# A block of the output projection in seven products of 128x128, and a new order of the instructions from the first load to the fourth block

## The chip, the core and the metric

The kernel runs on one core of one Trainium2 chip. The metric is the device time of one execution in microseconds (us). It was run three times; the median is 998.61 us (997.31 to 998.91). One execution was also taken with the profiler. All arithmetic is fp32.

## The reference

One cross-attention block. x has 16 batches of 1024 rows of 512 features, the context 16 batches of 64 rows.

```python
def _ada_ln(x, c, W_ss, b_ss):
    h = (x - mean(x)) / sqrt(var(x) + 1e-5)
    scale, bias = split(silu(c) @ W_ss + b_ss, 2)
    return (1 + scale)[:, None, :] * h + bias[:, None, :]

q      = _ada_ln(x,   cond, Wss_q,  bss_q)  @ Wq  + bq      # 16 heads of 32
k, v   = _ada_ln(ctx, cond, Wss_kv, bss_kv) @ Wkv + bkv
attn   = softmax(q @ k.T / sqrt(32))                        # per head, 64 keys
return x + ((attn @ v) @ Wp + bp)
```

## The kernel before, in words

**Blocks.** The rows of x are worked on in NB = 32 blocks of 512 rows (two per batch). The context is worked on once, in two groups of eight batches, "A" and "B", between the first blocks. Every block passes through these steps; the letters in brackets are the engines.

- `load_x` (SP issues the DMA), `q_stats` (VectorE: a batch-norm statistic and its aggregation per 128 rows, L287 and L288), `q_scale` (ScalarE and GpSimd: five and four instructions on 4 numbers a partition), `hidden` (ScalarE, L344: normalises), `turn` (VectorE, L374: 32x32 transposes), `move` (16 DMAs of 64 KB), `scale_features` (ScalarE, L459: the modulation).
- The query projection `query_product(i, 1..7)` (TensorE, L551). A 512x512x512 product would be eight products of 256x256x256. By Winograd's form of Strassen's method it is seven of them, `seven()`, with sums of weight blocks made once (`column_sums`) and sums of feature blocks made for every block (`feature_sums`, GpSimd, L510). Two of the seven, numbers 1 and 7, are cut in the same way a second time from the fifth block on, into seven products of 128x128x128: `quarter_products` in two parts of four and three (TensorE, L622), `feature_quarters` (GpSimd, L598 to L600, three sums), `quarter_copies` (ScalarE, L633) and `quarter_adds` (VectorE, L639 to L641). `query_out` (ScalarE, L662) and `query_added` (VectorE, L669) carry the results to SBUF.
- `score_products(i, 0)` and `(i, 1)` (TensorE, L755, 32x32 products into two PSUM tiles of two banks each, pool `ps_s`, which has two such tiles in all), `maximum` (VectorE, L772) and `copied` (ScalarE, L781), both reading these tiles; `maxima` (VectorE), `subtract` (GpSimd, L814: a whole 128x2048 tile), `weights` (ScalarE, the exponentials, L836), `swapped` (DMA), `again` (ScalarE, L861), `total` (GpSimd, L902), `row_total` and `inverse_rows` (VectorE, L907 and L922, then five small DMAs), `spread_rows` (VectorE, L957).
- `mix` (TensorE, L1002: weights times values), `divided` (VectorE, L981).
- The output projection `product(i, 1..7)` (TensorE, L1155): again seven products of 256x256x256, with the weight sums `WT` made once (`weight_sums`) and sums of rows for every block (`row_sum(i, 0..3)`, GpSimd, L1120 to L1127). Products 1, 6, 5, 3 add up in one PSUM bank, products 2, 4, 7 in another: `biased(i, 2)` and `biased(i, 3)` (ScalarE, L1099) set the banks to the bias, `output_seed` (ScalarE, L1108) copies the first bank into the second after product 1, and `added(i, n)` (VectorE, L1288) adds a bank to the residual rows; after products 3 and 4 the rows are stored by DMA.

A product of 256x256x256 is four fp32 matmuls of a 128x128 stationary block with 256 moving columns; the profile counts two instructions for each, eight in all. A cut product is seven fp32 matmuls of 128 moving columns, fourteen instructions.

**Order.** There is no scheduler: `tc.manual_schedule()` (L71) leaves every engine's queue in the order of the calls written out from L1297 on. Waits are put in where one instruction's bytes depend on another's, and every engine takes its own queue strictly in order. The calls are a way in (L1297 to L1757), a loop over blocks 3 to 29 (L1759), and a tail for blocks 30 and 31 (L1876 on). In the loop `i` is the block whose scores are made; `a = i - 1`, `b = i - 2`, `n = i + 1`, `f = i + 2`.

Some helpers stand in the file but are hardly used or not at all: `lowered(i, e)` (L816: half of the subtraction of the second score tile, on VectorE straight from PSUM; used for block 30 only), `subtract_half` (L822), `q_stats_two` and `q_square_mean` (L323, L336), and the family `inner_weight_sums`, `inner_biased`, `inner_quarters`, `inner_products`, `inner_copies`, `inner_adds` (L1181 to L1265).

Of the kernel before, what the change touches and what calls it, by code (L numbers as in the profile page):

```python
# [15 lines left out]
P = 128  # L16
# [4 lines left out]
def cross_attention_block(  # L21
# [18 lines left out]
    nc = tc.nc  # L40
# [5 lines left out]
    NC = H // P  # L46
# [141 lines left out]
    def load_projection(again=False):  # L188
        src = w_p.rearrange("(c p) o -> p c o", p=P)
        if again:  # L190
            nc.sync.dma_start(w_p_sb[:, : NC // 2, :], src[:, : NC // 2, :])
        else:
            nc.sync.dma_start(w_p_sb, src)
# [1104 lines left out]
    for _ in range(WARM):  # L1298
        nc.tensor.transpose(warm[:, :P], ident, ident)
    load_x('A')  # L1300
    load_scale_shift('kv', w_ss_kv, 0)
    q_stats('A', (0,))
    q_stats('A', (1,))
    q_stats('A', (2,))
    load_scale_shift('kv', w_ss_kv, 1)
    q_stats('A', (3,))
    q_scale('A')
    load_context_weights(1, 0)
    hidden('A', (0,))
    biases()  # L1310
    load_context_weights(0, 1)
    scale_shift_rows('kv', 0)
    scale_shift_taken('kv', 0)
    turned_features('A', 0)
    hidden('A', (2,))
    hidden('A', (1,))
    turned_features('A', 1)
    hidden('A', (3,))
    scale_shift('kv', 2 * NC, 0)
    turned_features('A', 2)  # L1320
    turned_features('A', 3)
    modulated('A', 0, 1, nc.vector)
    load_context_weights(0, 0)
    modulated('A', 0, 0, nc.scalar)
    scale_shift_rows('kv', 1)
    scale_shift_taken('kv', 1)
    load_x(0)
    modulated('A', 0, 0, nc.vector)
    modulated('A', 0, 1, nc.scalar)
    load_scale_shift('q', w_ss_q, 0)  # L1330
    column_sums('k', w_k_sb, w_k_sums, (0,))
    scale_shift('kv', 2 * NC, 1)
    load_scale_shift('q', w_ss_q, 1)
    column_sums('k', w_k_sb, w_k_sums, (1,))
    modulated('A', 1, 0, nc.scalar)
    column_sums('k', w_k_sb, w_k_sums, (2,))
    modulated('A', 1, 0, nc.vector)
    context_product('A', 'v', 1)
    context_product('A', 'k', 2)
    modulated('A', 1, 1, nc.vector)  # L1340
    load_x('B')
    modulated('A', 1, 1, nc.scalar)
    feature_sums('A', nc.vector, (0,))
    context_product('A', 'k', 1)
    feature_sums('A', nc.vector, (1,))
    context_out('A', 'k', 1)
    feature_sums('A', nc.vector, (2,))
    q_stats(0, (0,))
    context_out('A', 'k', 2)
    context_product('A', 'v', 2)  # L1350
    context_product('A', 'k', 6)
    q_stats(0, (1,))
    q_stats(0, (2,))
    scale_shift_rows('q', 0)
    q_stats(0, (3,))
    q_scale(0)
# [702 lines left out]
```

## Time and profile before

| | |
|---|---|
| median of the runs | 998.61 us |
| profiled execution, its own time | 996.79 us |
| its span | 994.9 us, so 1.9 us lie around the span |
| granted TensorE clock | 1.0 |
| TensorE busy | 982.9 us, 99% |
| VectorE busy | 898.5 us, 90% |
| GpSimd busy | 893.0 us, 90% |
| ScalarE busy | 780.2 us, 78% |
| DMA, written and read in all | 165.52 MB, mean 166 GB/s |
| one round of the loop (185.63 to 214.16 us and 470.85 to 499.37 us) | 28.5 us |
| loop over blocks 3 to 29 | 149.4 to 927.2 us |

The profiled execution took 1.8 us less than the median. Where an engine is nearly always busy, its idle time in a stage and what ended it are read from the waits; where it is not, busy shares say little. "PE" is TensorE, "PEld" its weight loads, "DVE" VectorE, "ACT" ScalarE, "POOL" GpSimd, "SPq" the queue of SyncE that issues DMAs. Neighbouring instructions on VectorE, ScalarE and GpSimd overlap by a little, so the spacing of their starts is often shorter than their duration.

### The profile page before, as it was taken

What the parts mean: (1) busy time and instruction counts of PE and PEld (TensorE: products, weight loads), DVE (VectorE), ACT (ScalarE), POOL (GpSimd) and SP (SyncE); (2) the same over time, 40 slices, a digit from 0 to 9 for tenths busy, and PEclk for the clock granted to TensorE, in tenths of its full rate; (3) what the DMA queues carried; (4) which work ended last, traced back from release to release, by engine and by line L of the source; (5) the groups of instructions that cost most, each with busy time, mean ns of one, the idle gap of its engine ahead of it and who ended that gap; (6) DMA issues with size and microseconds to landing.
All of it is one profiled execution on the core that took longest, in us unless ns stands there. A gap on an engine that the chain in (4) does not pass through costs nothing.

```text
span 994.9 us, 20661 instructions
## 1 busy us (share of the span) xinstructions
PE 982.9 (99%) x7501; PEld 767.7 (77%) x7501; DVE 898.5 (90%) x1326; ACT 780.2 (78%) x1169; POOL 893.0 (90%) x695
## 2 busy tenths in 40 slices
PE   8999999999999999999999999999999999999997
PEld 7888777777777777777777778777787787777776
DVE  7687899999999999999999999999999999987995
ACT  3878868888888888888888888888888888876540
POOL 2687999999999999999999999999999999999861
PEclk9999999999999999999999999999999999999999
DMA  9765755555656555556655555565555556544323
GB/s 316 257 173 148 172 161 143 156 161 171 190 181 181 164 152 164 142 180 191 184 178 159 160 154 151 182 188 181 178 152 172 149 155 182 148 135 131 116 90 108
DMA packets 114885, 165.52 MB, mean 166 GB/s; under 512 B 34872, under 2 KB 46160, under 8 KB 112864
## 3 DMA queue, kind: packets, MB, share of 16 engines
q1 hardware_dynamic: 114400, 163.67, 55.2%
q8 instruction: 60, 0.98, 0.4%
q0 software_dynamic: 384, 0.54, 0.2%
q14 instruction: 41, 0.34, 0.1%
HBM read 79.21 MB, written 34.60 MB: 114 GB/s over the span
## 4 chain that ended last, share of the span: by engine, by line
PE 94%; POOL 1%; DMA 1%; SPq 1%; DVE 1%; issue 1%; DVEq 0%; ACT 0%; POOLq 0%
PE pp L1155 37%; PE pq L551 29%; PE pq L622 10%; PE ps L755 7%; PE po L1002 6%; PE pk_A L551 1%; PE pv_B L551 1%; PE pk_B L551 1%; PE pv_A L551 1%; DMA w_k_sb<-in_L_xcond_Wkv_dram 1%; PE pp_0b L1155 1%; POOL sum L902 0%; SPq L166 0%; SPq L143 0%; DVE m L772 0%
## 5 line engine op out<-in xcount | busy, mean ns | idle before, releaser
L814 POOL TENSOR_TENSOR s<-s,mb 128x2048 f32<-128x2048 f32 x63 | 286.1, 4563 | 16.5 <-DVE mb L801 9.2
L1155 PE MATMUL pp<-w_p_sb,ot 128*128 128x256 f32 x756 | 178.9, 380 | 0.2 <-DVE ot L981 0.2
L772 DVE TRANSPOSE_TENSOR_REDUCE m<-ps 128x32 f32<-128x1024 f32 x128 | 152.3, 1226 | 10.0 <-PE ps L755 9.7
L781 ACT COPY s<-ps 128x1024 f32<-128x1024 f32 x126 | 127.4, 1013 | 41.8 <-PE ps L755 36.9
L1155 PEld LDWEIGHTS pp<-w_p_sb,ot 128*128 128x128 f32 x756 | 141.2, 190 | 21.9 <-issue 1.9
L662 ACT ACTIVATE qt<-pq,bias_t 128x256 f32<-128x256 f32 x256 | 107.5, 474 | 52.9 <-PE pq L622 27.8
L902 POOL TENSOR_TENSOR sum<-s,p 128x2048 f32<-128x2048 f32 x30 | 136.4, 4547 | 1.6 <-ACT p L836 1.6
L1288 DVE TENSOR_TENSOR r<-pp,r 128x512 f32<-128x512 f32 x188 | 123.6, 669 | 14.2 <-ACT xt L459 6.8
L551 PE MATMUL pq<-xt,w_q_sums 128*128 128x256 f32 x512 | 123.8, 385 | 0.0
L1155 PE MATMUL pp<-WT,ot 128*128 128x256 f32 x508 | 122.0, 383 | 0.0
L551 PEld LDWEIGHTS pq<-xt,w_q_sums 128*128 128x128 f32 x512 | 95.2, 190 | 34.3 <-issue 22.6
L1155 PE MATMUL pp<-WT,s 128*128 128x256 f32 x504 | 119.6, 380 | 0.7 <-DVE r L1288 0.5
L861 ACT ACTIVATE s<-s 32x2048 f32<-32x2048 f32 x60 | 114.6, 1910 | 1.5
L1155 PEld LDWEIGHTS pp<-WT,ot 128*128 128x128 f32 x508 | 94.2, 190 | 17.8 <-issue 3.0
L1155 PEld LDWEIGHTS pp<-WT,s 128*128 128x128 f32 x504 | 91.5, 191 | 11.9 <-DVE r L1288 1.4
L344 ACT ACTIVATE x<-x,rstdq 128x512 f32<-128x512 f32 x128 | 94.8, 807 | 1.0 <-POOL rstdq L305 0.9
L459 ACT ACTIVATE xt<-xt,ss_q 128x512 f32<-128x512 f32 x124 | 93.9, 807 | 0.5 <-DMA xt<-ht 0.3
L981 DVE TENSOR_TENSOR ot<-po,vb 128x1024 f32<-128x1024 f32 x64 | 75.5, 1219 | 18.8 <-PE po L1002 17.4
L287 DVE BATCH_NORM_STATS2 bs<-x 128x6 f32<-128x512 f32 x128 | 85.3, 666 | 0.0
L510 POOL TENSOR_TENSOR xt_sums<-xt 128x512 f32<-128x512 f32 x64 | 81.2, 1268 | 1.4 <-ACT xt L459 0.9
L374 DVE STREAM_TRANSPOSE ht<-x 128x512 f32<-128x512 f32 x124 | 77.7, 679 | 4.3 <-ACT x L344 2.2
L907 DVE TRANSPOSE_TENSOR_REDUCE lt<-sum 128x64 f32<-128x2048 f32 x31 | 71.6, 2310 | 6.2 <-POOL sum L902 3.9
(221 smaller groups left out, 1957.6 us busy)
## 6 DMA issues: line engine op xcount, KB each, us to landing
x<-in_x_dram SPq DMA_DIRECT2D x32, 1024.0 KB, 5.4
r<-in_x_dram SPq DMA_DIRECT2D x32, 1024.0 KB, 5.7
out_dram<-r SPq DMA_DIRECT2D x62, 512.0 KB, 5.0
xt<-ht SPq DMA_DIRECT2D x488, 64.0 KB, 2.0
p<-s SPq DMA_DIRECT2D x60, 256.0 KB, 3.8
wss_kv<-in_L_xcond_Wss_kv_dram SPq DMA_DIRECT2D x4, 512.0 KB, 7.2
wss_q<-in_L_xcond_Wss_q_dram SPq DMA_DIRECT2D x4, 512.0 KB, 10.5
vr<-ltd SPq DMA_DIRECT2D x128, 8.0 KB, 1.8
```

The source lines that it names most:

```text
L344: nc.scalar.activation(dst, src, AF.Identity, bias=rstd[:, 1, j : j + 1], scale=rstd[:, 0, j : j + 1])
L459: nc.scalar.activation(xt[:, :, c, :], xt[:, :, c, :], AF.Identity, scale=ss["q"][:, c, b : b + 1], bias=ss["q"][:, NC + c, b : b + 1],)
L551: nc.tensor.matmul(out_, lhsT=lhsT, rhs=rhs, start=new and m == 0 and c == 0, stop=c == HC - 1, skip_group_check=True,)
L622: nc.tensor.matmul(qa["q", k][:, q * P : (q + 1) * P], lhsT=lhsT, rhs=rhs, start=first and q == 0, stop=True, skip_group_check=True,)
L662: nc.scalar.activation(dst, src, AF.Identity, bias=bq_t[:, o : o + 1])
L772: nc.vector.tensor_reduce(m_tiles[i][:, z, 2 * e : 2 * e + 2, :], s_banks[i, z][e].rearrange("p r (j a) -> p r j a", a=32), AX.X, ALU.max, ...
L781: nc.scalar.copy(s_tiles[i, z][:, 2 * e : 2 * e + 2, :], s_banks[i, z][e])
L814: eng.tensor_tensor(s_tiles[i, z], s_tiles[i, z], mb_tiles[i], ALU.subtract)
L861: nc.scalar.activation(s_tiles[i, 0][at + 32 : at + 64], raw_tiles[i][at : at + 32], AF.Exp, scale=SCALE)
L902: nc.gpsimd.tensor_tensor(t, s_tiles[i, 0], s_tiles[i, 1], ALU.add)
L1155: nc.tensor.matmul(to, lhsT=rows[:, c, t * P : (t + 1) * P], rhs=cols[:, c, :], start=n == 2 and (i, 2) not in seeded and t == 0 and c == ...
L1288: nc.vector.tensor_add(r, a, r)
```

## The change

1. **Projection's product 1 is cut.** For blocks 2 to 28 (27 of the 32) `product(i, 1)` with `biased(i, 2)` gives way to `inner_biased`, `inner_quarters`, `inner_products` (two parts), `inner_copies` and `inner_adds`: seven products of 128x128x128. The sums of weight blocks are made once by `inner_weight_sums(1)` in the way in. One of them is written over a 128x128 block of the weights in place, so for blocks 29 to 31, which keep the whole product, `load_projection(again=True)` fetches that block (64 KB) once more in the tail.
2. **Work is moved between engines in every block from 3 on (statistics: from block 7 on).** Half of the subtraction of the second score tile goes from GpSimd to VectorE (`lowered(a, 0)`), which also saves one of the four `copied` on ScalarE; GpSimd keeps the other half (`subtract_half(a, 1, 1)`). The row statistics of two of the four row tiles go from VectorE to ScalarE (`q_stats_two`, two activations each whose elements are also summed up) with a small multiplication on GpSimd (`q_square_mean`).
3. **The order is another one throughout.** The way in is rewritten: the two halves of the keys' weights are loaded ahead of the first half of the values' weights, the first product of the context is the keys' product 1 in place of the values' product 1, and the order of blocks 0 to 4 is new. The loop now runs over blocks 5 to 27 and begins in the middle of a block's work; `load_x(i + 4)` and the statistics of block `i + 3` stand where those of `i + 5` and `i + 4` stood. The last four blocks are written out in the tail.

The functions of point 1, which were in the file already:

```python
def inner_weight_sums(v):              # POOL, once; s(2) is the weight block (1, 0) itself
    tt(s(0), w(1, 0), w(1, 1), ALU.add)
    tt(s(1), s(0), w(0, 0), ALU.subtract)
    tt(s(2), w(0, 0), w(1, 0), ALU.subtract)
    tt(s(3), w(0, 1), s(1), ALU.subtract)
    if v == 1:
        b = const.tile([P, HO], F32, tag="first", name="first_bias")
        nc.gpsimd.tensor_copy(b[:, :P], b_first[:, :P])
        tt(b[:, P:], b_first[:, P:], b_first[:, :P], ALU.subtract)
def inner_biased(i, v):                # ACT, two copies of 128x256
    nc.scalar.copy(acc[k][:, :HO], inner_bias[v])
    nc.scalar.copy(acc[k][:, HO:], zero.to_broadcast([P, HO]))
def inner_quarters(i, v, eng=nc.gpsimd):   # POOL; t shares its buffer with s2 of row_sum(i, 2)
    tt(t[:, 0:2], x[:, 1, 0:2, :], x[:, 0:2, 0, :], ALU.subtract)
    tt(t[:, 2], x[:, 1, 1, :], t[:, 0], ALU.subtract)
    tt(t[:, 3], x[:, 0, 1, :], t[:, 2], ALU.subtract)
def inner_products(i, v, first):       # PE
    todo = ((0, w(0, 0), x[:, 0, 0, :]), (2, s(0), t[:, 0]), (1, s(2), t[:, 1]), (3, s(1), t[:, 2])
            ) if first else ((0, w(0, 1), x[:, 0, 1, :]), (2, s(3), x[:, 1, 1, :]), (1, w(1, 1), t[:, 3]))
def inner_copies(i, v):                # ACT, 128x256
    nc.scalar.copy(inner_tiles[i, v][:, 0:2], a[:, :, 0, :])
def inner_adds(i, v):                  # DVE
    tt(t[:, 2], a[:, 3 * P :], t[:, 0], ALU.add)
    tt(both_, both_, t[:, 2:3].to_broadcast([P, 2, P]), ALU.add)
    tt(a[:, 3 * P :], a[:, P : 2 * P], t[:, 1], ALU.add)
def q_stats_two(i, ts):                # ACT, two per row tile
    nc.scalar.activation(junk, x, AF.Identity, scale=1.0 / H, accum_out=mv[:, t, 0:1])
    nc.scalar.activation(junk, x, AF.Square, scale=-1.0, bias=mv[:, t, 0:1], accum_out=mv[:, t, 1:2])
```

The core of the diff:

```diff
     def load_projection(again=False):
         if again:
-            nc.sync.dma_start(w_p_sb[:, : NC // 2, :], src[:, : NC // 2, :])
+            nc.sync.dma_start(w_p_sb[:, 0, P : 2 * P], src[:, 0, P : 2 * P])
...
-    load_context_weights(1, 0)
     hidden('A', (0,))
-    biases()
-    load_context_weights(0, 1)
+    hidden('A', (2,))
     scale_shift_rows('kv', 0)
     scale_shift_taken('kv', 0)
+    load_context_weights(0, 0)
     turned_features('A', 0)
...
+    scale_shift_rows('kv', 1)
+    load_context_weights(0, 1)
+    biases()
     hidden('A', (1,))
+    scale_shift('kv', 2 * NC, 0)
+    scale_shift_taken('kv', 1)
...
+    load_context_weights(1, 0)
+    scale_shift('kv', 2 * NC, 1)
+    modulated('A', 0, 0, nc.vector)
+    modulated('A', 1, 0, nc.vector)
...
-    context_product('A', 'v', 1)
-    context_product('A', 'k', 2)
...
     context_product('A', 'k', 1)
...
+    context_product('A', 'v', 2)
...
+    context_product('A', 'k', 2)
...
+    weight_quarter_sums(7)
+    inner_weight_sums(1)
...
-    for i in range(3, NB - 2):
+    for i in range(5, NB - 4):
         a, b, n, f = (i - 1, i - 2, i + 1, i + 2)
```

The loop after the change in full, its conditions (which hold in every round that they matter in) left out; several calls to a line:

```python
quarter_products(i, 7, True); lowered(a, 0); product(i-3, 3); product(i-3, 4); subtract(a, zs=(0,))
scale_features(n, (0,)); spread_rows(b); added(i-3, 3); scale_features(n, (1,)); mix(b)
quarter_copies(i, 7); quarter_adds(i, 7); added(i-3, 4); query_out(i, 6); hidden(f, (2,))
inner_biased(b, 1); weights(a, 0); quarter_products(i, 7, False); subtract_half(a, 1, 1); turn(f, (0,))
load_residual(a); feature_quarters(n, 1); weights(a, 1); query_product(i, 5); divided(b, (0,)); divided(b, (1,))
turn(f, (1,)); inner_quarters(b, 1); query_out(i, 7); total(a); turn(f, (2,)); q_stats_two(i+3, (0,))
inner_products(b, 1, True); inner_copies(b, 1); query_added(i, 5); turn(f, (3,)); load_x(i+4); inner_adds(b, 1)
query_product(i, 4); query_product(i, 3); query_added(i, 4); move(f, ks=(0,)); q_stats_two(i+3, (1,))
row_sum(b, 0); inner_products(b, 1, False); query_out(i, 3); scale_features(n, (2,)); output_seed(b)
q_stats(i+3, (2,)); swapped(a); scale_features(n, (3,)); score_products(i, 0); quarter_products(n, 1, True)
copied(i, 0, 1); q_stats(i+3, (3,)); q_square_mean(i+3, range(2)); row_total(a); quarter_copies(n, 1)
move(f, ks=(1,)); maximum(i, 0, 0); row_sum(b, 2); move(f, ks=(2,)); product(b, 2); quarter_adds(n, 1)
feature_sums(n, (0,)); move(f, ks=(3,)); product(b, 6); q_scale(i+3); copied(i, 0, 0); maximum(i, 0, 1)
hidden(i+3, (3,)); feature_sums(n, (1,)); feature_sums(n, (2,)); inverse_rows(a); quarter_products(n, 1, False)
added(b, 2); query_seed(n); score_products(i, 1); query_product(n, 2); added(b, 6); maximum(i, 1, 1)
maximum(i, 1, 0); biased(b, 3); row_sum(b, 3); maxima(i); again(a, 0); hidden(i+3, (0,)); row_sum(b, 1)
query_out(n, 2); product(b, 5); product(b, 7); added(b, 7); feature_quarters(n, 7); again(a, 1); added(b, 5)
feature_sums(n, (3,)); query_product(n, 6); hidden(i+3, (1,)); copied(i, 1, 1)
```

In the tail, three calls matter to the prediction:

```diff
     divided(y - 1, (1,))
-    query_product(z, 4)
+    load_projection(again=True)
+    query_product(z, 3)
...
     score_products(z, 0)
...
     product(y - 1, 1)
```

## The prediction on record

> **What bounds the kernel now.** I read the page first, then what TensorE waited for, then one round of the loop: busy times by stage, the chain that ended last, and the queues of the other engines.
>
> ```profile
> PE 982.9 (99%) x7501; PEld 767.7 (77%) x7501; DVE 898.5 (90%) x1326; ACT 780.2 (78%) x1169; POOL 893.0 (90%) x695
> PE 94%; POOL 1%; DMA 1%; SPq 1%; DVE 1%; issue 1%; DVEq 0%; ACT 0%; POOLq 0%
> ```
>
> TensorE is busy for 982.9 of 994.9 us and makes 94% of the chain that ended last. By what it waited for, the kernel has one longer stall, at the start; the second row matters further down:
>
> ```profile
> PE pc L210 <- DMA early<-in_cond_dram: 2.7, 1, 2.7
> PE pp L1155 <- POOL s L1125: 0.3, 1, 0.3
> ```
>
> The next view is busy time by stage, with one stretch of the way in and one round of the loop (length, then PE, PEld, DVE, ACT, POOL, each with its instructions, clock, DMA share, GB/s):
>
> ```profile
> 100.00:150.00 50.00, 49.72 (x356) 37.89 (x354) 43.98 (x61) 37.81 (x58) 48.49 (x29) 1.00 0.64 171
> 470.85:499.37 28.52, 28.52 (x221) 22.20 (x221) 26.96 (x39) 24.02 (x36) 27.48 (x22) 1.00 0.57 169
> ```
>
> In a round TensorE is busy for all of its 28.52 us. So a round becomes shorter only as TensorE's own work does, and only as far as the other queues can follow: VectorE and GpSimd have 1.6 and 1.0 us that are not busy, and a part of that is pauses between instructions. The chain through that round is TensorE alone and gives the price of each product (start, us, what):
>
> ```profile
> 474.30 0.89 PE pq L622 x8
> ...
> 478.64 0.67 PE pq L622 x6
> 479.31 1.88 PE po L1002 x32
> 481.19 1.93 PE pq L551 x8
> 483.11 1.73 PE pp L1155 x8
> ...
> 491.81 1.07 PE ps L755 x32
> ```
>
> **The change part by part: TensorE.** A whole product costs 1.73 us (483.11). A cut one costs 0.89 + 0.67 = 1.56 us (474.30 and 478.64, the 14 instructions of query product 7), though it does 7/8 of the arithmetic, which would be 1.51. The product after `mix` (481.19) shows 1.93 for 1.73: changing from small tiles to whole ones costs 0.20. A round keeps two scores and one `mix`, each followed by something large, so these costs stay; and in the new loop neither half of the cut projection product follows one, the first standing between `query_product` 5 and 4 and the second behind 3. The gain is 1.73 - 1.56 = 0.17 us a block, for 27 blocks **-4.6 us**, and a round of 28.35 us where nothing else is late.
>
> One row speaks to the obvious objection:
>
> ```profile
> L622 PEld LDWEIGHTS pq<-t_quarters,w_q_sb 128*128 128x128 f32 x224 | 29.5, 192 | 0.0
> ```
>
> Every instruction has its own weight load of 0.192 us, and 14 are more than 8. Yet eight follow each other in 0.89 us, 0.111 apiece, so loads overlap each other and the products. The Trainium skill, "TensorE: Matmul & The Clock Gate", section "Back-to-back issue gap", speaks against small products: pairs of load and product with 128 columns sustain about 81 ns where the product alone takes 56. Scaled by that ratio the isolated half of 0.216 us would be 0.156, 14 of them 2.2 us, and the change would cost about 0.45 us a block; the 0.111 of this trace disagrees, and I go by the trace.
>
> **The other engines in a round.** Prices from the groups by form (busy, mean ns of one):
>
> ```profile
> L814 POOL TENSOR_TENSOR s<-s,mb 128x2048 f32<-128x2048 f32 x63 | 286.1, 4563 | 16.5 <-DVE mb L801 9.2 <-ACT qt L662 7.2
> L598 POOL TENSOR_TENSOR t_quarters<-xt 128x256 f32<-128x256 f32 x28 | 20.5, 732 | 0.0
> L599 POOL TENSOR_TENSOR t_quarters<-xt,t_quarters 128x128 f32<-128x128 f32 x28 | 12.9, 460 | 2.2
> L902 POOL TENSOR_TENSOR sum<-s,p 128x2048 f32<-128x2048 f32 x30 | 136.4, 4547 | 1.6 <-ACT p L836 1.6
> L303 POOL TENSOR_SCALAR workq<-workq 128x4 f32<-128x4 f32 x33 | 6.3, 192 | 2.9
> L818 DVE TENSOR_TENSOR s<-ps,mb 128x1024 f32<-128x1024 f32 x2 | 2.4, 1220 | 0.1
> L781 ACT COPY s<-ps 128x1024 f32<-128x1024 f32 x126 | 127.4, 1013 | 41.8 <-PE ps L755 36.9 <-DVE m L772 3.9
> L633 ACT COPY t_quarters<-pq 128x256 f32<-128x256 f32 x56 | 21.0, 374 | 2.7 <-PE pq L622 1.8
> L344 ACT ACTIVATE x<-x,rstdq 128x512 f32<-128x512 f32 x128 | 94.8, 807 | 1.0 <-POOL rstdq L305 0.9
> L1099 ACT COPY pp<-b_p_sb 128x512 f32<-128x512 f32 x31 | 18.4, 593 | 0.2 <-DVE r L1288 0.2
> ```
>
> And VectorE's and GpSimd's queues in the same round (start, us; in brackets the idle time before):
>
> ```profile
> 473.63 9.08 POOL L814 TENSOR_TENSOR s<-s,mb 128x2048 f32<-128x2048 f32 x2 [0.32 <-ACT qt L662]
> 481.28 2.35 DVE L981 TENSOR_TENSOR ot<-po,vb 128x1024 f32<-128x1024 f32 x2 [0.65 <-PE po L1002]
> 483.55 2.48 DVE L374 STREAM_TRANSPOSE ht<-x 128x512 f32<-128x512 f32 x4
> 485.96 0.71 DVE L669 TENSOR_TENSOR qt<-pq,qt 128x256 f32<-128x256 f32 x2
> 486.60 0.67 DVE L287 BATCH_NORM_STATS2 bs<-x 128x6 f32<-128x512 f32 x1
> 487.31 0.18 DVE L288 BATCH_NORM_AGGREGATE mvq<-bs 128x2 f32<-128x6 f32 x1
> 489.87 2.31 DVE L907 TRANSPOSE_TENSOR_REDUCE lt<-sum 128x64 f32<-128x2048 f32 x1
> 492.22 0.55 DVE L922 RECIPROCAL lt<-lt 128x64 f32<-128x64 f32 x1
> 493.07 2.38 DVE L772 TRANSPOSE_TENSOR_REDUCE m<-ps 128x32 f32<-128x1024 f32 x2 [0.30 <-PE ps L755]
> 495.38 0.25 DVE L639 TENSOR_TENSOR t_quarters<-pq,t_quarters 128x128 f32<-128x128 f32 x1
> 496.34 0.68 DVE L1288 TENSOR_TENSOR r<-pp,r 128x512 f32<-128x512 f32 x1
> ```
>
> GpSimd waits 0.32 us a round, so its queue fills 28.52 - 0.32 = 28.20. The change takes half a subtraction, 4.56/2 = 2.28, and adds the three sums of `inner_quarters`, 0.73 + 2 x 0.46 = 1.65 and some 0.15 of pauses, and a small multiplication, 0.19: 28.20 - 2.28 + 1.80 + 0.19 = **27.9 of 28.35**. VectorE waits 0.65 + 0.30, so its queue fills 27.57. It gains `lowered`, 1.22, and `inner_adds`, which by L639 to L641 (495.38 to 496.34) is 0.96; it loses two statistics, 0.67 + 0.18 each: 27.57 + 1.22 + 0.96 - 1.70 = **28.05 of 28.35**. ScalarE has 28.52 - 24.02 = 4.5 us free; it loses one copy (1.01), gains 2 x 0.37 - 0.59 = 0.15 in the bias, 0.37 in `inner_copies`, and four activations of 128x512. No activation in this trace also sums its elements; the bounds are a plain copy of that size (0.59) and L344's activation with a further 0.3 for fetching the sum (1.1). I take L344's 0.81, the same shape: 24.02 + 0.15 + 0.37 - 1.01 + 3.24 = **26.8 of 28.35**; at 1.1 it would be 27.9. All three fit, VectorE barely.
>
> Fitting is not enough, since each queue is strictly in order and the change adds waits. `inner_copies` waits for the first half of the products; behind it on ScalarE are two statistics and `query_out(i, 3)`, which the scores need. `inner_adds` waits for that copy; behind it `row_total` and both `maximum`. `inner_quarters` waits for `divided`; behind it GpSimd's `total`. The tightest loop I find runs from the second score, over TensorE to the end of `mix`, then down VectorE's queue to the second `maximum`, which frees the PSUM tile that the next second score writes. TensorE's part: 1.07 + 1.93 + 1.73 x 3 + 0.89 + 1.73 x 2 + 1.88 = 14.42. VectorE's part by the spacing of starts in that queue: `divided` 2.27, three `turn` 1.81, two `query_added` 1.28, `inner_adds` 0.96, two statistics 1.70, `row_total` 2.35, two `maximum` 2.38, `quarter_adds` 0.96, in all 13.71; with 0.1 for handing over, **28.2, under 28.35 by 0.1**. `row_total` needs GpSimd's `total`: from the end of `mix` half of `divided` (1.2), `inner_quarters` (1.8) and L902's 4.55 make 7.5, and VectorE gets to `row_total` after 8.0, so that `total` is in time by half a microsecond.
>
> **The way in.** At 15.39 TensorE begins the context with the values' product 1, then stops for the keys' weights:
>
> ```profile
> 9.01 8.78 DMA w_k_sb<-in_L_xcond_Wkv_dram
> 15.39 2.02 PE L551 MATMUL pv_A<-w_v_sb,xk_A 128*128 128x256 f32 x8 [0.22 <-DVE xk_A L431]
> 17.92 3.69 PE L551 MATMUL pk_A<-xk_A,w_k_sb 128*128 128x256 f32 x16 [0.51 <-DMA w_k_sb<-in_L_xcond_Wkv_dram]
> ```
>
> The third half-matrix in SP's queue lands at 17.79, whichever it is. In the new order the first product is the keys', whose half comes first, and the second is the values' 2, whose half now lands at 17.8: the same wait at the same place. Ahead of that, VectorE now modulates only after the second half of scale and shift, one more pass from PSUM through TensorE and back; I put that at 0.7 us (0 if the halves come together, 1.5 if the second comes as much later as a half-matrix takes to follow another here). The wait of 0.51 hides so much of it: **+0.2**, between 0 and 1.0.
>
> From 100 to 150 us GpSimd is busy 48.49 of 50, and it cost TensorE 0.3 (`pp <- POOL s`). Into this stretch come `inner_weight_sums`, six small sums of about 0.46 or 2.8 us, block 2's `inner_quarters` (1.8), and four sums of the query weights that stood earlier (1.8); block 3's half subtraction (2.28) goes. That is 4.1 more against 1.5 us of free time: between 0 (later order covers it) and 2.6 us. I take **+1.0**, nearer the row that shows GpSimd's queue costing 0.3.
>
> **The tail.** The reload of 64 KB stands on SP behind the last reader of that weight block (block 28's products) and ahead of `inverse_rows(y)`:
>
> ```profile
> xt<-ht SPq DMA_DIRECT2D x488, 64.0 KB, 2.0
> ```
>
> It lands in about 2.0 us, and ahead of the product that reads it TensorE still has a product and a score (1.73 + 1.07); its issue comes earlier than these. So it costs nothing; were SP late, up to 2 us. The other steps of the tail stay in kind, and I put their new order at 0, give or take 1.5: a row of the trace for it there is none, and 1.5 is about one product that stands idle or is covered.
>
> **Sum**: -4.6 + 0.2 + 1.0 = **-3.4 us**, that is 993.4 for the profiled execution's 996.79. This execution took 1.8 less than the median of 998.61, so against the median it is **995.2**.
>
> **The rivals.** *Nothing to be measured.* TensorE's gain is there but way in and tail give it back: GpSimd's 2.6 and a tail 1.5 longer leave -0.3. For it: a queue of 99% in the way in. Against it: TensorE's total wait there was 0.3. 998.3.
>
> *VectorE becomes the bound, and the kernel slower.* The tight loop above has 0.1 us to spare, and from there on every delay on it lengthens each round. `inner_copies` stands behind two summing activations on ScalarE; at 1.1 for 0.81 it hands `inner_adds` on 0.6 later, and a round takes 28.8 if VectorE has nothing to put in between. The half microsecond of `total` is the next to go. With 0.5 of delay a round is 28.7 and 23 rounds lose 0.35 each against 28.35: +8.0 on the forecast, 1003. For it: 28.05 of 28.35 full. Against it: `turn` and `query_added` stand ahead of `inner_adds` and absorb a late copy, and ScalarE has 1.5 us of free time a round at 0.81.
>
> *Weight loads bound the small products.* Only if the loads of the projection's sums do not overlap as those of the query's do: 14 x 0.192 = 2.69 for 1.73, +0.96 x 27 = +26 us in place of -4.6, 998.6 + 26 + 1.2 = 1026. The 0.111 us speak against it. This is where the Trainium skill's sustained gap, cited above, belongs.
>
> **How the numbers follow.** The forecast, from a way in without any stall and a shorter tail (-4.6 - 1.5 = -6.1, 992.5) to 2 us under the median: 0.60, own range 992.2 to 996.6. Nothing to be measured: 0.20. VectorE: 0.18. Weight loads: 0.02. A measurement of this kernel can tell about 0.2%, 2 us, from no change. So faster 0.60, same 0.20, slower 0.20. The range reaches from 992.2 to 1001.5, half way into VectorE's case; about 1 in 10 lies beyond each end.
>
> **What would show it.** Right: a round at 28.3 to 28.4 us with TensorE busy throughout, the cut product's halves at 0.89 and 0.67, the queue of VectorE nearly full and ScalarE busy for about 27. Wrong: the loop at 28.5 or more with TensorE waiting in every round at the second score for `maximum` (VectorE's case) or at the row sums' products for GpSimd; waits of more than 2 us between 100 and 180 us (way in); or the summing activations above 1.1 us.

## The result, and the profile after

The changed kernel takes **1068.55 us** (median of 1063.55 to 1084.85) against 998.35 for the kernel before, measured beside it: a ratio of **1.0688, interval 1.0648 to 1.0727**. The execution of 1084.85 us was in a slower state than the others and is left out of the ratio. The prediction was 995.2 with a range up to 1001.5, so it had the sign wrong and the range missed by 67 us. The profiled execution took 1069.53 us with a span of 1067.7, that is 72.8 more than before. Unless another kernel is named, "after" is this execution.

The page's busy times and the chain by engine:

```profile
PE 1011.5 (95%) x7663; PEld 789.6 (74%) x7663; DVE 912.9 (85%) x1334; ACT 833.5 (78%) x1396; POOL 885.2 (83%) x807
PE 46%; DVE 15%; DMA 14%; SPq 14%; issue 7%; POOL 2%; ACT 1%; DVEq 0%; POOLq 0%; ACTq 0%
```

No engine is the bound any more. TensorE's share of the chain fell from 94% to 46%, and VectorE, DMAs and SP's queue, with 1% each before, have 43% together. Three of the largest waits lie on the path that the rest of this section follows (engine, waiting and releasing line: us in all, times, longest):

```profile
DVE vb L957 <- DMA vr<-ltd: 65.9, 26, 5.6
ACT pp L1205 <- DVE r L1288: 62.8, 24, 5.1
...
PE pq L622 <- DVE pq L641: 33.1, 20, 4.3
```

`spread_rows` (L957, it reads the reciprocals of the softmax sums) waits in 26 blocks for the small DMAs of `inverse_rows`. That wait was 1.1 us in all before. Behind it in VectorE's queue stand `added(i-3, ..)`, which ScalarE waits for, and `quarter_adds(i, 7)`, which TensorE waits for. In the kernel before, `quarter_adds` stood ahead of `spread_rows` (504.69 and 505.68 us in one round).

`spread_rows` comes once a block and so divides the span. Its start for blocks 3 and 25 was 192.78 and 819.44 us before, 206.32 and 885.15 after. So of the 72.8 us the way in has 13.5, the 22 rounds between have 678.83 - 626.66 = **52.2** (30.86 us a round for 28.48) and the rest has 182.55 - 175.46 = 7.1. Those 22 rounds by engine, in after:

```profile
206.32:885.15 678.83, 646.94 (x4961) 505.20 (x4946) 604.12 (x858) 577.88 (x970) 596.85 (x551) 0.99 0.52 156
```

VectorE is busy for 89% of this, GpSimd for 88%, ScalarE for 85%: the three queues that the prediction filled up by hand are not full. The one that it did not look at is SP's. SP's queue in one round after (start, us, what; "x12" are twelve DMAs):

```profile
527.24 0.38 SPq L119 DMA_DIRECT2D x<-in_x_dram  x1
529.28 2.41 SPq L399 DMA_DIRECT2D xt<-ht  x4
531.73 2.30 SPq L841 DMA_DIRECT2D p<-s  x2
534.08 7.58 SPq L399 DMA_DIRECT2D xt<-ht  x12
542.06 0.79 SPq L925 DMA_DIRECT2D ltd<-lt  x1
544.14 1.75 SPq L927 DMA_DIRECT2D vr<-ltd  x4
```

And before, from the exchange of the exponentials on:

```profile
489.86 1.15 SPq L841 DMA_DIRECT2D p<-s  x2
491.10 9.01 SPq L399 DMA_DIRECT2D xt<-ht  x12
500.21 0.53 SPq L925 DMA_DIRECT2D ltd<-lt  x1
501.89 1.75 SPq L927 DMA_DIRECT2D vr<-ltd  x4
503.98 2.41 SPq L399 DMA_DIRECT2D xt<-ht  x4
```

Before, twelve of a block's sixteen `move` DMAs went ahead of the reciprocals (L925, L927) and four behind them. In the new order all sixteen go ahead, and they begin only when `query_product(i, 3)` has freed the buffer that they write (L399 waits 45.6 us in all for it). What follows is a closed loop through VectorE and back to TensorE. The round's links on VectorE and TensorE, in after:

```profile
529.05 0.38 PE L1246 MATMUL pp<-w_p_sb,ot 128*128 128x128 f32 x2
...
547.22 2.31 DVE L957 STREAM_TRANSPOSE vb<-vr 128x2048 f32<-128x2048 f32 x1 [1.65 <-DMA vr<-ltd]
...
550.81 0.30 DVE L641 TENSOR_TENSOR pq<-pq,t_quarters 128x128 f32<-128x128 f32 x1
...
551.26 0.46 PE L622 MATMUL pq<-xt_sums,w_q_sums 128*128 128x128 f32 x2 [0.39 <-DVE pq L641]
...
557.18 1.89 PE L551 MATMUL pq<-xt,w_q_sums 128*128 128x256 f32 x8
558.90 0.38 PE L1246 MATMUL pp<-w_p_sb,ot 128*128 128x128 f32 x2
```

`query_product(i, 3)` ends where the cut product's second half (L1246) begins, at 529.05. SP's moves, the exchange, the reciprocals and their landing take until 547.22 (18.2 us); `spread_rows`, `added` and `quarter_adds` until 551.26 (4.0); the rest of the quarter products, three query products (5, 4 and 3) and the cut product's first half, up to the end of `query_product(.., 3)` at 558.90 (7.6). Together 29.85 us. Nothing in this loop is a full engine; a round cannot be shorter than the loop, and TensorE's 28.35 no longer counts.

### The profile page after: what moved, and what is told of

The parts are those of the page before. It is cut to its first block, busy times and chain, and to the rows that moved or that the text cites. A ratio compares the mean times of both kernels' runs of the same rounds, so it can differ in the third digit from the quotient of the medians.

```text
span 1067.7 us, 21512 instructions
## 1 busy us (share of the span) xinstructions
PE 1011.5 (95%) x7663; PEld 789.6 (74%) x7663; DVE 912.9 (85%) x1334; ACT 833.5 (78%) x1396; POOL 885.2 (83%) x807
## 4 chain that ended last, share of the span: by engine, by line
PE 46%; DVE 15%; DMA 14%; SPq 14%; issue 7%; POOL 2%; ACT 1%; DVEq 0%; POOLq 0%; ACTq 0%
PE pq L551 15%; PE pp L1155 15%; SPq L399 9%; PE ps L755 4%; DMA ltd<-lt 4%; DMA x<-in_x_dram 4%; DMA vr<-ltd 4%; PE pq L622 4%; DVE r L1288 4%; PE pp L1246 3%; SPq L927 3%; DVE ot L981 2%; DVE ht L374 2%; DVE m L772 2%; PE po L1002 1%
## 5 line engine op out<-in xcount | busy, mean ns | idle before, releaser
L814 POOL TENSOR_TENSOR s<-s,mb 128x2048 f32<-128x2048 f32 x36 | 163.8, 4554 | 13.2 <-DVE mb L801 9.3
L662 ACT ACTIVATE qt<-pq,bias_t 128x256 f32<-128x256 f32 x256 | 106.2, 465 | 41.5 <-PE pq L551 39.0
L1155 PE MATMUL pp<-w_p_sb,ot 128*128 128x256 f32 x540 | 127.9, 380 | 2.6 <-ACT pp L1099 2.1
L957 DVE STREAM_TRANSPOSE vb<-vr 128x2048 f32<-128x2048 f32 (+1 forms) x33 | 74.0, 2243 | 65.9 <-DMA vr<-ltd 65.9
L551 PE MATMUL pq<-xt,w_q_sums 128*128 128x256 f32 x512 | 129.6, 399 | 0.1
L1155 PEld LDWEIGHTS pp<-w_p_sb,ot 128*128 128x128 f32 x540 | 99.8, 190 | 18.2 <-ACT pp L1099 3.4
L551 PEld LDWEIGHTS pq<-xt,w_q_sums 128*128 128x128 f32 x512 | 100.4, 201 | 15.6 <-DVE qt L669 1.2
L344 ACT ACTIVATE x<-x,rstdq 128x512 f32<-128x512 f32 x128 | 103.2, 813 | 7.0 <-POOL rstdq L305 6.0
L781 ACT COPY s<-ps 128x1024 f32<-128x1024 f32 x99 | 98.6, 1000 | 9.8 <-DVE m L772 3.3
L1155 PEld LDWEIGHTS pp<-WT,s 128*128 128x128 f32 x504 | 95.3, 190 | 14.7 <-issue 0.8
L459 ACT ACTIVATE xt<-xt,ss_q 128x512 f32<-128x512 f32 x124 | 97.5, 810 | 9.3 <-DMA xt<-ht 3.5
L1155 PEld LDWEIGHTS pp<-WT,ot 128*128 128x128 f32 x508 | 94.3, 190 | 13.5 <-ACT pp L1099 1.6
L374 DVE STREAM_TRANSPOSE ht<-x 128x512 f32<-128x512 f32 x124 | 83.0, 689 | 7.5 <-DMA V_A<-stage_A 3.2
L801 DVE STREAM_TRANSPOSE mb<-m 128x2048 f32<-128x2048 f32 x32 | 74.0, 2312 | 1.1
```

What stands on the lines that cost most here:

```text
L344: nc.scalar.activation(dst, src, AF.Identity, bias=rstd[:, 1, j : j + 1], scale=rstd[:, 0, j : j + 1])
L374: nc.vector.transpose(ht_tiles[i][:, :, :, t, :].rearrange("p k c b -> p c k b"), x_tiles[i][:, t, :].rearrange("p (c k b) -> p c k b", c= ...
L459: nc.scalar.activation(xt[:, :, c, :], xt[:, :, c, :], AF.Identity, scale=ss["q"][:, c, b : b + 1], bias=ss["q"][:, NC + c, b : b + 1],)
L551: nc.tensor.matmul(out_, lhsT=lhsT, rhs=rhs, start=new and m == 0 and c == 0, stop=c == HC - 1, skip_group_check=True,)
L662: nc.scalar.activation(dst, src, AF.Identity, bias=bq_t[:, o : o + 1])
L781: nc.scalar.copy(s_tiles[i, z][:, 2 * e : 2 * e + 2, :], s_banks[i, z][e])
```

## The experiments

Three theories at the outset, numbered as the expectations number them. **1, SP's order:** the reciprocals stand behind the moves, and that wait is the loss. **2, the cut product:** its waits (`inner_quarters`, `inner_copies`, `inner_adds`) are. **3, too much work:** VectorE and ScalarE have more to do since statistics and half of the subtraction moved. Every kernel was timed beside the kernel before on the same chip (medians of 997.0 to 998.4 us, so two rows of the table compare to about a microsecond). The last column is the mean round from block 3 to block 25 in the profiled execution (before 28.48, after 30.86).

| | median us | ratio to before, interval | round |
|---|---|---|---|
| after | 1068.55 | 1.0688 (1.0648 to 1.0727) | 30.86 |
| whole_product | 1077.12 | 1.0789 (1.0744 to 1.0834) | 31.16 |
| inverse_early | 1082.40 | 1.0840 (1.0807 to 1.0872) | 31.27 |
| x_load_late | 1043.59 | 1.0454 (1.0429 to 1.0478) | 29.96 |
| before_moves_first | 1045.22 | 1.0483 (1.0461 to 1.0504) | 30.26 |
| inverse_on_act | 1030.92 | 1.0327 (1.0303 to 1.0351) | 29.43 |
| both_moved | 1029.14 | 1.0309 (1.0287 to 1.0331) | 29.22 |
| late_readers | 1051.06 | 1.0536 (1.0518 to 1.0554) | 30.03 |
| late_readers_x_late | 1050.32 | 1.0525 (1.0509 to 1.0540) | 30.03 |
| reads_later | 1017.50 | 1.0202 (1.0183 to 1.0220) | 28.76 |
| whole_second | 1034.86 | 1.0377 (1.0355 to 1.0400) | 29.46 |
| quarters_first | 1022.52 | 1.0247 (1.0222 to 1.0272) | 28.83 |
| way_in | 1015.18 | 1.0165 (1.0146 to 1.0185) | 28.64 |
| way_in_two | 1017.11 | 1.0202 (1.0183 to 1.0221) | 28.61 |
| small_products | 993.06 | 0.9958 (0.9945 to 0.9970) | 28.41 |

**The kernel before with all moves ahead of the reciprocals** (before_moves_first)

```diff
         row_total(i)
+        if i + 3 < NB:
+            move(i + 3, ks=(3,))
         inverse_rows(i)
-        if i + 3 < NB:
-            move(i + 3, ks=(3,))
```

> The kernel before with one call moved in its loop: the last four moves of a round ahead of inverse_rows, not behind it. Theory 1: its spread_rows starts right when the reciprocals land, so four moves of 0.6 to 0.75 us ahead of them delay it by 2.4 to 3.0 us, of which VectorE's wait for mix hides 0.65; the round goes from 28.5 to about 30.5, and the kernel to 1040 to 1060 us, without any cut product. Theories 2 and 3: nothing of the kind is in this kernel, so no change, 998 us.

Four DMAs exchanged with five make the tuned kernel 47.6 us slower, with no cut product in it. SP in one of its rounds:

```profile
511.80 11.48 SPq L399 DMA_DIRECT2D xt<-ht  x16
523.38 0.52 SPq L925 DMA_DIRECT2D ltd<-lt  x1
525.05 1.75 SPq L927 DMA_DIRECT2D vr<-ltd  x4
```

`spread_rows` waits 60.6 us there. The order on SP alone gives a loss of the size of the one to be explained.

**The changed kernel with product 1 whole again** (whole_product): `inner_biased(b, 1)` becomes `biased(b, 2)`, `inner_products(b, 1, True)` becomes `product(b, 1)`, and `inner_quarters`, `inner_copies`, `inner_adds`, the second half and `inner_weight_sums(1)` go.

> The changed kernel with the whole product 1 back in blocks 2 to 28 (no cut product, no sums for it), its order and everything else kept. Theory 1, SP's queue: the reciprocals of the row sums leave SP behind twelve moves, come back late and hold spread_rows; the cut product has little to do with it. Then the loop keeps a round of 30 to 31 us; the chain is shorter only by the sums on GpSimd, so 1050 to 1068 us. Theory 2, the cut product itself is what costs (its waits for sums, copy and adds, and the matmuls around it): then about 1000 us and a round near 28.5.

It is slower by 8.6 us, outside the range of either theory, and the wait for the reciprocals is still 61.8 us. The second theory falls. SP's moves wait longer here for the load of x, 40.5 us in all for 29.7 in after (a wait that x_load_late takes up below); whether that is the 8.6 us was not tried.

**Reciprocals ahead of the twelve moves in the changed kernel** (inverse_early)

```diff
             row_total(a)
+        if i >= 4:
+            inverse_rows(a)
...
-        if i >= 4:
-            inverse_rows(a)
```

> The changed kernel with one call moved in the loop: inverse_rows right behind row_total, so that its five DMAs stand ahead of the twelve moves on SP, not behind them. Theory 1: spread_rows waits for nothing any more, the round falls to 28.5 to 29.5 us (the moves now land 4 us later, and scale_features may wait for them), 1010 to 1040 us. Theory 2 and theory 3 (VectorE and ScalarE have too much work since the statistics and half of the subtraction moved): no change, 1065 us or so.

This missed: the wait for the reciprocals went, as foreseen, and the kernel became slower still. Two waits of this kernel tell why:

```profile
ACT xt L459 <- DMA xt<-ht: 86.3, 26, 4.5
...
DVE vb L957 <- DMA vr<-ltd: 7.0, 3, 3.6
```

In the new order two readers of SP's transfers stand at the head of the next round, `spread_rows` and the first `scale_features` (L459). While SP stands at the reciprocals' way through memory the moves are late instead. Exchanging the two only chooses who waits, so the theory has to be put wider: what SP has to do between `query_product(i, 3)` and the start of the next round is too much for the time there.

**The 1 MB load of x behind the reciprocals** (x_load_late): `load_x(i + 4)` moves from ahead of `move(f, ks=(0,))` to behind `inverse_rows(a)`.

> The changed kernel with the 1 MB load of x behind inverse_rows in the loop, not ahead of the moves. Theory 1 in the form that the moves are slow to issue because the load is ahead of them in the same DMA queue: the twelve moves then take about 7.5 us in every round (now 7.6 to 11), the round loses 1 to 2 us, 1025 to 1050 us. If the load is not what slows them: no change, 1060 to 1070.

25.0 us less. The load costs SP 0.38 us to issue, but the twelve moves behind it take 9.5 us on the mean of the loop's rounds and up to 12.2, against 8.4 and up to 9.3 here. SP's own waits say why (after, then x_load_late):

```profile
SPq L399 <- DMA x<-in_x_dram: 29.7, 20, 3.9
SPq L399 <- DMA x<-in_x_dram: 7.3, 4, 2.6
```

In these traces SP's DMAs use eight semaphores in turn, and each move that waits is the eighth DMA behind the load: it takes the load's semaphore over and waits until the 1 MB has landed, though it reads no byte of it. So not every wait in these queues is for bytes. In the 22 rounds of after this makes 22.3 us, 1.0 a round, about what the mean round has over the 29.85 us shown above; in x_load_late none of it falls into the loop. It fits the wider theory: not the place of one instruction, but the sum of what SP does and waits for there.

**The reciprocals off SP** (inverse_on_act). In the loop, ScalarE issues the write where `inverse_rows(a)` stood and the four reads behind `again(a, 0)`.

```diff
+    def inverse_written(i):
...
+        nc.scalar.dma_start(d.rearrange("c a r j -> (c a) r j"), lt)
...
+    def inverse_read(i):
...
+            nc.scalar.dma_start(v[32 * r : 32 * r + 32], d[:, :, r, :].rearrange("c a j -> a c j"))
...
-            inverse_rows(a)
+            inverse_written(a)
...
         again(a, 0)
+        inverse_read(a)
```

> The five small DMAs of the reciprocals leave SP's queue in the loop: ScalarE issues the write where the reciprocals stood, and the four reads two instructions later. The 16 moves and everything else stay. Theory 'SP's queue, the reciprocals stand behind the moves': the reciprocals land some 5 us earlier, spread_rows no longer waits, nothing else was late, and 22 rounds of 30.86 us fall to 28.4 to 28.8: about 1018 us (1010 to 1030). Rival 'the moves end too late whoever stands behind them': the wait passes to scale_features, as it did when the reciprocals were put ahead of the moves: rounds of 30 us or more, 1045 or over.

37.6 us less, short of the 50 that were expected, and the rounds are uneven. `spread_rows` waits 5.2 us in all. What is left shows on ScalarE. It can issue the reads only when the write has landed, spends 2.0 us a round on issuing the four, and is idle for 22.2 us in all before its next instruction (lines behind L932 are 16 higher in the kernels with this edit; L973 is `spread_rows`):

```profile
ACT x L344 <- DMA vr<-ltd: 22.2, 21, 2.7
...
DVE vb L973 <- DMA vr<-ltd: 5.2, 3, 2.8
```

**The same with the load of x late** (both_moved).

> The same and the 1 MB load of x behind the moves in SP's queue. Theory of the reciprocals' place: with that wait gone the load's place is worth little, within 8 us of the kernel with the reciprocals on ScalarE alone, about 1012. Rival: the moves are the limit, so the load's place is worth as much as it was alone, about 25 us.

1.8 us less, within the spread of the runs. The load's place was worth 25 us while the reciprocals stood behind the moves and is worth nothing measurable once they do not: one loss, with two ways of relieving it, not two losses.

**The four reads two instructions later on ScalarE** (reads_later): `inverse_read(a)` from behind `again(a, 0)` to behind `query_out(n, 2)`.

> Reciprocals issued by ScalarE and the load of x behind the moves, as in the kernel with both moved, but the four reads of the reciprocals stand behind query_out(n, 2), two instructions later, so that ScalarE does not sit on the landing of the write (it waited 24 us in all there). If that wait made the long rounds (29 to 30 us beside tight ones of 28.6 to 28.8): all rounds near 28.7 and about 1019 us. If something else does: within 4 us of 1029.

As expected: 1017.5, and the rounds are even, 28.6 us but for a few. The 22 rounds of this kernel:

```profile
207.99:840.62 632.63, 627.47 (x4933) 494.85 (x4926) 602.12 (x858) 572.28 (x966) 591.38 (x550) 1.00 0.55 167
```

TensorE is busy for 99% again. 46.2 of the loop's 52.2 us are gained back by taking five small DMAs out of SP's queue, moving one load and placing the reads where ScalarE need not wait for the write. This settles the loop's loss but for 6 us. Theory 3 falls with it, since VectorE and ScalarE still do all that was moved to them.

**The readers later instead** (late_readers, and late_readers_x_late with the load behind the moves): reciprocals on SP ahead of the twelve moves; `scale_features(n, (0,))` and `(1,)` behind `weights(a, 1)`, `feature_quarters(n, 1)` behind `total(a)`.

> The reciprocals stay on SP, ahead of the 12 moves, and the readers of the moved rows come later: the first two scale_features behind weights on ScalarE and feature_quarters(n, 1) behind total on GpSimd. Theory 'two readers of SP's work stand at the start of a round, and SP can serve one of them in time': with both served, rounds of 28.4 to 29, about 1020 us. Rival 'SP as a whole is too slow for a round (31 us of issues and waits)': rounds stay at 30.5 or more, 1060 or over.

> The same with the load of x behind the moves. If the two early readers were all: within 8 us of the kernel without this step. If the moves' speed behind the 1 MB load still counts: 10 to 25 us less.

17.5 us less than after, not 48; the load of x is worth nothing here; and nearly every round takes 30.0 us. SP is out of the loop here (7.6 us of waits for the moves, 9.1 for the reciprocals), but the two scalings now delay `query_out(i, 7)` on ScalarE, and TensorE waits 0.8 us a round for it at `query_product(i, 4)`. The edit made a new loop of its own, so it tells of the old one only that it could be opened at the readers too.

**What the cut product is worth to TensorE** (small_products): the kernel before, with seven plain 128x128x128 products in place of product 1 of blocks 2 to 28. It leaves out the sums, copies and additions, so its output is another one.

```diff
-        product(a, 1)
+        small_products(a)
```

> The kernel before with nothing changed but product 1 of blocks 2 to 28: at its place and in its bank, seven products of 128x128x128 one behind the other, of plain blocks of rows and weights, without the sums, copies and additions that Strassen's form needs (the values are other ones; biased and output_seed stay whole). It is TensorE's price of the cut product by itself. Prediction's step, 1.56 for 1.73 us: 4.6 us faster than before, 993. Other theory, from a tight round of the mended order, where the halves and what they slow down take 1.79: within 2 us of before or up to 2 slower.

4.6 us faster, by the interval 3.0 to 5.5: the prediction's term, its last digit by luck. Most rounds take the 28.35 us that were foreseen (28.41 on the mean). The products in its trace:

```profile
482.42 1.73 PE L1266 MATMUL pp<-w_p_sb,ot 128*128 128x128 f32 x14
483.98 1.89 PE L551 MATMUL pq<-xt_sums,w_q_sb 128*128 128x256 f32 x8
```

From 482.42 to 483.98 is 1.56 us for the fourteen instructions. The rate that the prediction took from the Trainium skill ("TensorE: Matmul & The Clock Gate", section "Back-to-back issue gap") and scaled to 2.2 us does not apply to these.

**And in the new order** (whole_second): reads_later with `product(b, 1)` whole, where the cut product's second half stood.

> The same with product 1 whole, for blocks 2 to 28, at the place of the cut product's second half. What the cut product is worth on TensorE. Prediction's step: the cut saves 0.17 a block, so this is 4.6 us slower than the kernel it is made from. Other theory, from a tight round of 28.81 us: the halves take 0.93 and 0.76 of it with what follows them slowed by 0.10, and the score right behind the second half takes 1.38 for 1.07, because it waits for query_out(i, 3), which 1.73 us of whole product would cover; the cut then costs 0.2 to 0.4 a block and this kernel is 5 to 10 us faster.

17.4 us slower, against both theories. With the first half gone, `query_product(i, 4)` follows `query_product(i, 5)` at once and waits for its bank: TensorE waits 14.7 us in all there for `query_out` (L662). So what the cut product is worth in the new order stays open: here and in whole_product, taking it out brought other waits. What the run does show is the score: with a whole product between it and `query_product(i, 3)` it takes 1.07 us (605.66 to 606.73). In reads_later, where only the second half stands between, it takes 1.39:

```profile
591.13 1.89 PE L551 MATMUL pq<-xt,w_q_sums 128*128 128x256 f32 x8
592.85 0.38 PE L1262 MATMUL pp<-w_p_sb,ot 128*128 128x128 f32 x2
...
593.61 1.45 PE L755 MATMUL ps<-qt,K_B 32*32 32x512 f32 x32
595.00 0.49 PE L622 MATMUL pq<-xt,w_q_sb 128*128 128x128 f32 x2
```

The score waits for `query_out(i, 3)`, which 0.76 us of small products do not cover and 1.73 did. **The first part of `quarter_products(n, 1)` ahead of the score** (quarters_first) was to fill that gap.

> The kernel with the reads later, with the first part of quarter_products(n, 1) ahead of score_products(i, 0) instead of behind it, so that TensorE has 0.9 us of work between the cut product's second half and the score that waits for query_out(i, 3). If the score's 1.38 us is that wait: a round 0.3 shorter, 7 us faster. If it is the price of small tiles behind small products: no difference over 2 us.

5.0 us slower. The score is back at 1.07, so the 0.32 was a wait; but the quarter products write a bank that the same `query_out` frees, and TensorE waits for it there (6.7 us in all, 24 times). The place of the wait changed, not the wait.

**The way in** (way_in): reads_later with the reciprocals of blocks 1 to 3 on ScalarE, the loads of x for blocks 6 and 8 further back, and the exchange of block 1 ahead of the moves.

> The kernel with the reads later, with the same edit in the way in: reciprocals of blocks 1 to 3 issued by ScalarE, the loads of x for blocks 6 and 8 behind (most of) the moves of blocks 4 and 6, and the exchange of the exponentials of block 1 ahead of the moves. There the fourth block's spread_rows starts at 208.0 us, against 192.8 in the kernel before. If SP's queue is the cause of the lost time from 100 us on: 5 to 8 us less, 1010 to 1013. If the way in loses its time by its own order of products and waits for ScalarE: within 2 us of 1017.5.

2.3 us less: block 3's `spread_rows` starts at 206.41 us for 207.99. **The two longest waits there taken away** (way_in_two):

> The kernel of way_in, with its two longest waits of TensorE between 60 and 160 us taken away: the load of x for block 3 behind the moves of block 1 (context product B, keys 1 waits 2.1 us for ScalarE, which sits on the moved rows of block 1), and for block 4 the first two scale_features behind the exponentials of block 2 and block 6's first statistic behind spread_rows(1) (product 1 of block 1 waits 3.0 us for its bias, and after that pause the granted clock is 0.5 for some 3.5 us). If these waits for SP's transfers are the way in's loss: 2.1 + 3.0 + 1.6 for the clock, about 1008 to 1010. If other waits were just as near behind them: within 2 us of 1015.

Nothing gained. Both waits went and others of 1.75 and 3.08 us stood in their places (a score for ScalarE's copy, product 1 of block 1 for `divided(1)`). So SP's waits, as far as they were taken away here, have a small part in the way in's 13.5 us. The rest looks like an order in which several engines are late by about as much; which changes of that order cause it stays open.

## Why the prediction was wrong, point by point

**The step that failed** is "All three fit, VectorE barely" and the search for "the tightest loop I find" behind it. Three queues were added up, VectorE, GpSimd and ScalarE, and SP's was taken up only for the tail's reload of 64 KB. The change put the last four of a block's moves, too, ahead of the reciprocals, and that stood in the loop as it was written out: `move(f, ks=(3,))`, then `inverse_rows(a)`, then `spread_rows(b)` at the head of the next round. SP's part could be had from rows of before: twelve moves 9.01, four more 2.41, the exchange 1.15, the reciprocals 0.53 and 1.75 with 1.15 between them, 16.0 in all. With the rows of before for the other links as well (landing 1.4, VectorE 3.9, TensorE 6.8) the loop comes to about 28.1: as tight against 28.35 as the loop that the prediction found, a warning but not yet the loss. With after's own landing (1.3) and links (4.0 and 7.6) it is 28.9. In the traces it took 29.85 in the round shown and 30.86 on the mean, the last microsecond being the moves' wait for the load of x, which no row of the loop before showed.

**TensorE as the bound; the cut product's 4.6 us.** Both right where nothing else is late: 1.56 us and 4.6 by small_products. In the new order the halves are followed at once by what they were priced for (0.89 and 0.76 in reads_later, the second up to the score), but the round is 28.6 there, not 28.35. The prediction left out that the second half takes the place of 1.73 us of product between `query_product(i, 3)` and the score; the score's 0.32 is more than the 0.17 gained. Its reading that two scores and one `mix` are "each followed by something large" does not fit either order (before, both scores are followed by quarter products of 128x128; in the new one `mix` and the first score are), but no term of its sum rests on that.

**The three queues that were added up** hold. After, the summing activations take 0.63 + 0.19 and 0.72 + 0.19 us with the fetch of the sum, on the mean 0.86 (0.81 taken, 1.1 the bound); `lowered` 1.215; half a subtraction 2.386 (2.28 taken).

```profile
L825 POOL TENSOR_TENSOR s<-s,mb 128x1024 f32<-128x1024 f32 x27 | 64.4, 2386 | 1.3 <-ACT s L781 1.3
L332 ACT ACTIVATE squares<-x,mvq 128x512 f32<-128x512 f32 x50 | 36.1, 722 | 1.6
L818 DVE TENSOR_TENSOR s<-ps,mb 128x1024 f32<-128x1024 f32 x29 | 35.2, 1215 | 2.2 <-ACT s L861 2.1
L331 ACT ACTIVATE squares<-x 128x512 f32<-128x512 f32 x50 | 31.3, 627 | 0.0
...
L331 ACT ACTIVATION_READ_ACCUMULATOR squares<-x 128x1 f32 x50 | 9.6, 192 | 0.0
L332 ACT ACTIVATION_READ_ACCUMULATOR squares<-x,mvq 128x1 f32 x50 | 9.3, 187 | 0.0
```

With SP out of the way (reads_later) VectorE is busy for 95% of the rounds and TensorE still for 99%. Neither rival on the slower side came about, VectorE as the bound or the weight loads. The loss had a third cause, which stood in none of the cases.

**The way in**, priced at +1.2, shows +13.5 by block 3. Its start cost 1.4 us instead of 0.2, by the second half of scale and shift that comes later, as was named. The five first products of the context were done at 25.00 before; in after TensorE waits for that half and is done with them at 26.4:

```profile
13.62 1.07 PE L248 MATMUL ps_kv<-wss_kv,early 128*32 128x128 f32 x28 [1.01 <-DMA wss_kv<-in_L_xcond_Wss_kv_dram]
...
24.66 1.89 PE L551 MATMUL pk_A<-xk_sums_A,w_k_sums 128*128 128x256 f32 x8
26.48 1.28 PE L248 MATMUL ss_q<-wss_q,early 128*32 128x128 f32 x36
```

The rest was missed: up to block 3's `spread_rows` TensorE is idle for 13.55 us (192.77 busy of 206.32) against 4.75 (188.03 of 192.78). That is 8.8 of the 13.5; the other 4.7 are busy time, in which TensorE has 27 more instructions ahead of this mark than before. "Waits of more than 2 us between 100 and 180 us" was named as a sign, with GpSimd's queue as its cause. One of 2.13 us came, and all of TensorE's waits of that stretch (4.9 us) were for ScalarE, none for GpSimd. The "queue of 99%" there is TensorE's row; GpSimd's 48.49 of 50 us are 97%.

**The tail**, 0 give or take 1.5, shows 7.1 after block 25, but only 1.7 in reads_later (177.18 for 175.46): its first rounds were still SP's.

## What to carry to other kernels

When a change reorders a loop, write out SP's queue as carefully as an engine's: what each DMA waits for, also by a semaphore that it takes over from an earlier one, how long the ones ahead of it take (sixteen of 64 KB took 10 to 15 us here, such waits included), and who reads what comes last. Then look for closed loops, from a buffer that is freed to the transfer that fills it, to its reader, and back to the instruction that frees it; their length is a bound on the round even where no engine is full. Small products are worth their arithmetic only where what they replace was not covering someone's wait.

## What the runs showed of the hardware

**A pause of TensorE can cost more than its length.** Where TensorE stood for 4.33 us in after, the products behind it ran at half the clock. The same product that takes 1.73 us (552.00 to 553.73) took 3.41:

```profile
400.21 0.77 PE L622 MATMUL pq<-xt_sums,w_q_sums 128*128 128x128 f32 x2 [4.33 <-DVE pq L641]
...
401.62 3.62 PE L551 MATMUL pq<-xt,w_q_sums 128*128 128x256 f32 x8
405.03 0.63 PE L1246 MATMUL pp<-w_p_sb,ot 128*128 128x128 f32 x2
```

The stretches of that time (the granted clock is the third number from the end):

```profile
400.21:403.50 3.29, 3.29 (x11) 2.93 (x12) 3.29 (x5) 3.29 (x3) 2.60 (x5) 0.50 0.77 296
403.50:406.00 2.50, 2.50 (x11) 2.14 (x10) 1.87 (x5) 2.17 (x7) 2.42 (x3) 0.57 0.45 111
406.00:410.00 4.00, 4.00 (x23) 3.59 (x22) 3.55 (x10) 1.92 (x6) 4.00 (x3) 1.00 0.86 320
```

The length of a pause does not decide this alone. In after a pause of 1.93 us (up to 582.66) was followed by half the clock, and the product behind it took 3.19 us; others of 2.06, 2.13 and 2.20 us were not. In x_load_late one of 3.37 us (up to 210.11) was not. The traces show where the difference lies: the granted clock changes only at multiples of 3.41 us from one another, and half the clock lasted 3.41 or 6.83 us each time. So time can be cut into windows of 3.41 us by these changes. These are the windows around the 1.93 us in after, then around the 3.37 us in x_load_late (length, then TensorE's busy time first):

```profile
579.74:583.15 3.41, 1.48 (x28) 0.60 (x13) 3.34 (x7) 1.57 (x3) 0.74 (x2) 1.00 0.20 79
583.16:586.56 3.40, 3.40 (x11) 2.82 (x10) 3.40 (x5) 3.40 (x4) 2.64 (x6) 0.50 0.60 229
...
205.16:208.57 3.41, 1.58 (x32) 0.31 (x16) 2.49 (x2) 2.16 (x5) 1.92 (x1) 1.00 0.02 2
208.57:211.98 3.41, 1.87 (x12) 1.77 (x13) 3.34 (x7) 2.95 (x4) 1.66 (x3) 1.00 0.53 206
```

The 1.93 us fall into one window, the 3.37 us into two, with 1.8 us idle in the first. In all runs, start and end left out, each of the 33 windows at full clock in which TensorE was idle for 2.0 us or more was followed by half the clock. Of those with less than 1.89 us idle only one was (1.41 us, in late_readers_x_late), and the few between went either way. The Trainium skill ("TensorE: Matmul & The Clock Gate", "Part 1: The HAM clock gate") puts this at about 3.4 us of idling, and about as long to come back; the 3.41 us at half clock agree with the way back, the 1.93 us of idling do not agree with the way down.

**How long SP takes over DMAs within the chip's own memory varies.** Twelve moves of 64 KB took from 7.6 to 12.2 us in the rounds of after (11.17 in the one with the pause above), and 7.6 to 9.3 with the 1 MB load behind them. At 7.58 us (534.08) each takes about 0.6. A part of the rest is the wait for the landing of the load; single moves that took up to 1.9 us, also with the load behind them, no run here explains.
